# Experts with 128-slot tiles, two tiles in a turn

## The chip, the cores and the metric

The kernel runs on one core of a Trainium2 chip. The metric is the time of one execution on the device, in microseconds (us). Times of a kernel are given as the median of several runs; the profile comes from one further execution of its own.

## The reference

The input x is (8, 256, 32, 32): eight batches of 256 channels and 1024 positions. Layer 0 is a deformable convolutional attention with a small MLP for the position bias; layer 1 is an attention with sigmoid weights, followed by a mixture of experts. The change concerns the mixture most:

```python
x = x + conv_attention(group_norm(x))              # layer 0
t = tokens(x)                                      # 1024 tokens of 256 a batch
t = t + sigmoid_attention(layer_norm(t))           # layer 1
u = layer_norm(t)

logits = u @ router_w.T                            # 8 experts
probs = softmax(logits)
rw, re = top_k(probs, 2)
rw = rw / rw.sum(-1)
out = u
for e in range(8):
    h = gelu(u @ w1[e] + b1[e])
    out = out + combine[:, e] * (h @ w2[e] + b2[e])
t = t + out
```

`combine` is zero but for the two experts that each token has chosen. So each batch has 2 x 1024 pairs of a token and an expert. All arithmetic is fp32.

## The kernel before

**The outer order.** A Python loop writes out 8 x 64 turns (L1053), and a last pass, `in_order`, ties each engine to the order in which its instructions were written. Batch b of the loop does the position-bias MLP of batch b: in each turn two first layers (`first_layer`, on VectorE L451 or GpSimd L453), two second layers on TensorE (L466, with a relu on ScalarE L472 or a maximum on VectorE L474) and, every second turn, four rows of the third layer (L493). The tables that the first layer reads (`ta`, `nb`) are made by `terms`: every eighth turn (0, 8, 16, ...) four DMAs on the SyncE queue (L423, L424), three turns later a scaling (L427 on ScalarE, L428 on VectorE), one more turn later a small matmul (L434).

**What is woven in.** Each turn also advances, behind its MLP work:

- `prep` of the next batch: group norm, query projection, the depthwise convolution, offsets, sampling (L227 to L403);
- `attention` of layer 1, in two halves: `upper` starts at turn 53 of its own batch, `rest` runs in the next batch. `rest` ends with `route` (L780), which takes the logits to slots, and with sixteen scatters by GpSimd (L763), in turns 41 and after;
- `experts` (L867), the mixture of a batch; `mix` (L1038) says in which turns one step of it is made;
- `combine` (L937), 22 steps in consecutive turns from the one in which a mixture ends: sixteen gathers by GpSimd (L965) from the experts' rows `ys`, the weighted sums (L957), transposes (L948) and the output.

**The slots.** `route` counts, for each expert, how many tokens chose it, gives each expert as many tiles of SLOTS = 256 rows as it needs, and each pair a row in one of its expert's tiles. `need`, `ends`, `at`, `place`, `slot` are those steps; `which` and `whose` give `expert`, the expert of each tile. Whatever the counts are, TILES = (2048 + 8 x 255) // 256 = 15 tiles are enough, and always 15 are computed. The scatters write the normalized tokens to `xs`, of which there are two.

**One round.** `experts` is a generator with software pipelining. Step n of its loop (L890) makes, in this order: the second matmul of tile n - 2 (`yp`, L896, eight matmul records), the bias and the write to `ys` (L901, L904); the fetch of tile n + 2 (`xl`, L874); the load of the weights of tile n + 1 (`weights`, L877: one read of the expert's number into a register of SyncE, then w1 with b1, 257 KB, L880, and w2 with b2, 384 KB, L882); the first matmul of tile n - 1 (`hp`, L916, eight records) and its Gelu (`ht`, L922); four transposes of tile n (`tp`, L929) and their copy (`xg`, L931). In fp32 one matmul call makes two records in the trace. `wpool` holds three buffers for each weight. Before the loop there are two steps with fetches alone, so a mixture takes 19 steps.

**When.** The mixture of batch b is made in the loop of batch b + 2: at turns 24 and 26 and at odd turns from 27 on but for 35, 37, 39, 61 and 63, which are sixteen steps; the last three fall in batch b + 3, at turns 3, 7 and 9. Batches 0 and 1 have no mixture steps, and turns 3 and 7 of batch 2 have none. In batch 7 mixture 5 is made at odd turns and those divisible by three from 11 to 37. Mixture 6 begins in turns 62 and 63 and goes on while `rest` of batch 7 is made without an MLP beside it; mixture 7 comes after the last scatter and is made beside the combine of batch 6. The combine of batch 7 ends the program.

**Memory.** `low` (eleven buffers of 128 x 512) serves `xl`, `xg`, `ht`, `yt` and others; constants come as one tile `cs` of NCST columns, 799.5 KB, at the start.

Of the kernel before, what the change touches and what calls it, by code (L numbers as in the profile page):

```python
# [27 lines left out]
SLOTS = 256  # L28
TILES = (2 * N + E * (SLOTS - 1)) // SLOTS

# [8 lines left out]
    ("ident", 128), ("gavg", 128), ("base", 512), ("basef", 128),  # L39
    ("gq", 1), ("cx", 1), ("cy", 8), ("rev", 64),  # L40
    ("ones", 128), ("before", 128), ("full", 256), ("tiles", (E - 1) * TILES), ("form", 12),
# [53 lines left out]
def tile_conv_attn_hybrid(ctx: ExitStack, tc: tile.TileContext, x, par, qw, w1, w2_, cst, out):  # L95
# [9 lines left out]
    wpool = ctx.enter_context(tc.tile_pool(name="w", bufs=3))  # L105
# [105 lines left out]
    xss = [nc.dram_tensor(f"xs{n}", [TILES * SLOTS, C], F32, kind="Internal").ap() for n in range(2)]  # L211
# [15 lines left out]
    def prep(b, xb, st):  # L227
# [41 lines left out]
        for t in range(KS * KS):  # L269
# [9 lines left out]
        oa = one.tile([P, 2, NJ], F32, name="oa")  # L279
        nc.scalar.activation(  # L280
            oa.rearrange("p k (y x) -> p k y x", x=8), oc.rearrange("p (y k) x -> p k y x", k=2), AF.Gelu
        )
# [4 lines left out]
        for g in range(2):  # L287
            for c in range(2):
                nc.tensor.matmul(
                    op.rearrange("p (c k g j) -> p c k g j", c=2, k=2, g=2)[:, c, :, g, :],  # L290
                    lhsT=pw[:, 2 * g + c : 2 * g + c + 1].to_broadcast([P, P]), rhs=oa, start=True, stop=True,
                )
        opf = psum("opf")
        nc.tensor.matmul(
            opf[:, 0:128].rearrange("p (k j) -> p k j", k=2),
# [6 lines left out]
        nc.vector.scalar_tensor_tensor(gk[:, 0:512], gk[:, 0:512], 4.0, base, ALU.mult, ALU.add)  # L302
# [7 lines left out]
        fl = one.tile([P, 2 * NJ], F32, name="fl")  # L310
# [9 lines left out]
        fr = one.tile([P, 2, 64], F32, name="fr")  # L320
# [22 lines left out]
        hx = one.tile([P, 256], F32, name="hx")  # L343
# [238 lines left out]
    def attention(b, st, o, rt):  # L582
# [152 lines left out]
        def rest():  # L735
# [21 lines left out]
            yield from route(lqs, rt)  # L757
# [22 lines left out]
    def route(lqs, rt):  # L780
# [6 lines left out]
        revv = rev.rearrange("p (m e) -> p m e", e=E)  # L787
# [14 lines left out]
        def pick(name):  # L802
# [28 lines left out]
        nc.tensor.matmul(cnt, lhsT=cst_("ones"), rhs=sums, start=False, stop=True, skip_group_check=True)  # L831
        need = one.tile([P, E, E, 4], F32, name="need")
        nc.vector.tensor_tensor(
            need, cnt[:, 8, :].unsqueeze(1).unsqueeze(3).to_broadcast([P, E, E, 4]),
            cst_("full").rearrange("p (e f n) -> p e f n", e=E, f=E), ALU.is_gt,
        )
        nc.vector.tensor_reduce(ends[:, 1:9], need.rearrange("p e f n -> p e (f n)"), AX.X, ALU.add)
        for c in range(2):
# [4 lines left out]
            at, ends[:, 0:8].unsqueeze(1).to_broadcast([P, 8, E]), float(SLOTS), cnt[:, 0:8, :], ALU.mult, ALU.add  # L843
        )
        place = one.tile([P, 2, 8], F32, name="place")
        for c, oh in enumerate((oh1, oh2)):
# [5 lines left out]
        which = one.tile([P, TILES, E - 1], F32, name="which")  # L852
        nc.vector.tensor_tensor(
            which, ends[:, 1:8].unsqueeze(1).to_broadcast([P, TILES, E - 1]),
            cst_("tiles").rearrange("p (t e) -> p t e", e=E - 1), ALU.is_le,
# [11 lines left out]
    def experts(b, rt):  # L867
        xs = rt["xs"]
        yv = dram.tile([TILES * SLOTS, C], F32, name="ys")
        tiles = {}  # L870

        def fetch(t):
            xl = low("xl")
            nc.sync.dma_start(out=xl, in_=xs[t * SLOTS : (t + 1) * SLOTS, :].rearrange("(s p) c -> p s c", p=P))  # L874
            tiles[t] = [None, None, xl]

        def weights(t):  # L877
            e = nc.sync.value_load(rt["expert"][0:1, t : t + 1], min_val=0, max_val=E - 1)
            f1 = wpool.tile([P, 2 * C + 2], F32, name="w1")
            nc.sync.dma_start(out=f1, in_=w1[bass.ds(e, 1)].rearrange("e p c -> (e p) c"))  # L880
            f2 = wpool.tile([P, 3 * C], F32, name="w2")
            nc.sync.dma_start(out=f2, in_=w2_[bass.ds(e, 1)].rearrange("e p c -> (e p) c"))  # L882
            tiles[t][0:2] = f1, f2
# [4 lines left out]
        weights(0)  # L888
        yield
        for n in range(TILES + 2):  # L890
            if n >= 2:
                _, f2, ht = tiles.pop(n - 2)
                yp = psum("yp").rearrange("p (s c) -> p s c", s=2)
                for s in range(2):
                    for f in range(2):
                        nc.tensor.matmul(  # L896
                            yp[:, s, :], lhsT=ht[:, f, s * P : (s + 1) * P], rhs=f2[:, f * C : (f + 1) * C],
                            start=(f == 0), stop=(f == 1),
                        )
                yt = low("yt")  # L900
                nc.vector.tensor_tensor(  # L901
                    yt, yp, f2[:, 2 * C :].unsqueeze(1).to_broadcast([P, 2, C]), ALU.add
                )
                nc.sync.dma_start(  # L904
                    out=yv[(n - 2) * SLOTS : (n - 1) * SLOTS, :].rearrange("(s p) c -> p s c", p=P), in_=yt
                )
            if n + 2 < TILES:
                fetch(n + 2)
            if n + 1 < TILES:
                weights(n + 1)  # L910
            if 1 <= n <= TILES:
                f1, _, xg = tiles[n - 1]
                hp = psum("hp").rearrange("p (f i) -> p f i", f=2)
                for f in range(2):
                    for k in range(2):
                        nc.tensor.matmul(  # L916
                            hp[:, f, :], lhsT=f1[:, k * C + f * P : k * C + (f + 1) * P], rhs=xg[:, k, :],
                            start=(k == 0), stop=(k == 1),
                        )
                ht = low("ht")  # L920
                for f in range(2):
# [307 lines left out]
```

## Time and profile before

| | us |
|---|---|
| median of 3 runs | 3216.83 |
| lowest, highest | 3212.77, 3220.61 |
| the profiled execution, its own time | 3218.55 |
| its span, first to last instruction | 3216.8 |

The mean granted TensorE clock was 0.974 of full speed. By the view of busy time in stretches, the batches of the loop took 278, 337, 368, 376, 379, 375, 379 and 392 us, after a start of 73; the end, after turn 63 of batch 7, took 260 us.

| group | count | busy us | mean ns |
|---|---|---|---|
| L466 second MLP layer, TensorE | 8192 | 1026.8 | 611 |
| L493 third MLP layer, TensorE | 4096 | 506.5 | 613 |
| L896 `yp`, TensorE | 960 | 241.8 | 396 |
| L916 `hp`, TensorE | 960 | 229.4 | 382 |
| L929 `tp`, TensorE | 480 | 73.9 | 277 |
| L922 `ht`, ScalarE | 240 | 100.8 | 471 |
| L901 `yt`, VectorE | 120 | 82.6 | 688 |

Matmuls are pipelined, so the mean of one record is longer than the distance of two starts; busy time counts overlapping records once. The trace moved 281.20 MB by DMA in all, 87 GB/s on average.

### The profile page before, as it was taken

How to read it: one execution, taken by the hardware profiler on the slowest of the kernel's cores; microseconds unless marked ns; L12 is line 12 of the kernel's file. 1: busy time of each engine (PE TensorE's matmuls, PEld its weight loads, DVE VectorE, ACT ScalarE, POOL GpSimd, SP SyncE). 2: the span in 40 equal slices, each digit the busy share in tenths (PEclk: the TensorE clock that was granted, in tenths of full speed). 3: DMA queues.
4: the chain of work that ended last, by engine and by line, in shares of the span. 5: the costliest groups of instructions: out<-in, count | busy, mean ns of one | idle time of the engine just before them, and what ended most of it. 6: DMA issues, size and time to landing. Idle time of an engine off the chain costs nothing. (4 is left out here: it accounts for less than half of the span.)

```text
span 3216.8 us, 50328 instructions
## 1 busy us (share of the span) xinstructions
PE 2928.8 (91%) x19468; PEld 1465.1 (46%) x19468; DVE 2173.7 (68%) x2996; ACT 1841.1 (57%) x2435; POOL 1547.5 (48%) x945
## 2 busy tenths in 40 slices
PE   3888998899999998999989999999999999988986
PEld 2223343334545454554535445354544546523765
DVE  4898678967785787756876587757777464586122
ACT  3666565656566556655566566655566566545322
POOL 2546344744464454634555365543646343364123
PEclk7999999999999999999999999999999999999998
DMA  3311101210344123432335224441234333532277
GB/s 100 89 32 45 21 19 27 69 29 19 85 122 129 32 65 98 136 91 50 87 88 145 55 61 103 117 133 33 66 90 141 81 84 97 147 96 64 66 248 235
DMA packets 421567, 281.20 MB, mean 87 GB/s; under 512 B 283088, under 2 KB 378064, under 8 KB 421328
## 3 DMA queue, kind: packets, MB, share of 16 engines
q1 hardware_dynamic: 408752, 242.80, 28.4%
q0 software_dynamic: 12288, 33.57, 3.4%
q8 instruction: 153, 2.51, 0.3%
q10 hardware_dynamic: 288, 1.62, 0.1%
q14 instruction: 86, 0.70, 0.1%
HBM read 204.51 MB, written 73.40 MB: 86 GB/s over the span
## 5 line engine op out<-in xcount | busy, mean ns | idle before, releaser
L453 POOL TENSOR_TENSOR h<-ta,nb 128x1024 f32<-128x1024 f32 x512 | 1060.7, 2073 | 1122.9 <-PE h2p L466 1052.8
L466 PE MATMUL h2p<-h,pr__97 64*64 64x512 f32 x8192 | 1026.8, 611 | 118.8 <-DVE h L474 86.8
L474 DVE TENSOR_TENSOR h<-h2p,nc 128x1024 f32<-128x1024 f32 x512 | 624.2, 1219 | 518.0 <-PE h2p L466 512.4
L472 ACT ACTIVATE h<-h2p,pr__97 128x1024 f32<-128x1024 f32 x512 | 569.7, 1113 | 516.0 <-PE h2p L466 514.9
L451 DVE TENSOR_TENSOR h<-ta,nb 128x1024 f32<-128x1024 f32 x512 | 765.3, 1495 | 0.7 <-ACT ta L427 0.5
L458 ACT ACTIVATE h<-h 128x1024 f32<-128x1024 f32 x512 | 536.8, 1049 | 82.8 <-POOL h L453 82.7
L466 PEld LDWEIGHTS h2p<-h,pr__97 64*64 64x64 f32 x8192 | 256.1, 133 | 639.9 <-issue 303.6
L493 PE MATMUL sim<-h,pr__97 128*32 128x512 f32 x4096 | 506.5, 613 | 0.0
L493 PEld LDWEIGHTS sim<-h,pr__97 128*32 128x32 f32 x4096 | 108.6, 111 | 375.4 <-issue 375.4
L896 PE MATMUL yp<-w,ht 128*128 128x256 f32 x960 | 241.8, 396 | 18.7 <-ACT tn L630 10.7
L701 PE MATMUL ap<-qt,tn 128*128 128x256 f32 x1024 | 250.5, 388 | 0.5 <-ACT nc L439 0.5
L715 PE MATMUL vp<-tt,sg 128*128 128x256 f32 x1024 | 243.3, 381 | 0.3 <-ACT sg L706 0.3
L922 ACT ACTIVATE ht<-hp,w 128x256 f32<-128x256 f32 x240 | 100.8, 471 | 239.9 <-PE hp L916 200.6
L916 PE MATMUL hp<-xg,w 128*128 128x256 f32 x960 | 229.4, 382 | 6.0 <-ACT gk L299 2.8
L965 POOL DMA_INDIRECT gs<-ys,slot x128 | 139.1, 1087 | 193.2 <-DMA ys<-yt 57.8
L701 PEld LDWEIGHTS ap<-qt,tn 128*128 128x128 f32 x1024 | 185.2, 190 | 88.5 <-issue 55.9
L896 PEld LDWEIGHTS yp<-w,ht 128*128 128x128 f32 x960 | 178.8, 195 | 85.1 <-issue 31.8
L715 PEld LDWEIGHTS vp<-tt,sg 128*128 128x128 f32 x1024 | 193.2, 190 | 33.2 <-issue 6.9
L901 DVE TENSOR_TENSOR yt<-yp,w 128x512 f32<-128x512 f32 x120 | 82.6, 688 | 176.6 <-PE yp L896 137.9
L916 PEld LDWEIGHTS hp<-xg,w 128*128 128x128 f32 x960 | 183.0, 191 | 33.3 <-ACT gk L299 3.7
L763 POOL DMA_INDIRECT xs<-ut,slot x128 | 166.9, 1304 | 47.9 <-DVE slot L850 26.2
L276 DVE SCALAR_TENSOR_TENSOR oc<-qp,pr__97,oc 128x128 f32<-128x128 f32 x280 | 168.7, 603 | 7.2
(264 smaller groups left out, 2550.6 us busy)
## 6 DMA issues: line engine op xcount, KB each, us to landing
w<-in_w SPq DMA_DIRECT2D x120, 384.0 KB, 3.9
ta<-fd SPq DMA_DIRECT2D x128, 256.0 KB, 5.5
w<-in_w SPq DMA_DIRECT2D x120, 257.0 KB, 3.2
xl<-xs SPq DMA_DIRECT2D x120, 256.0 KB, 3.0
ys<-yt SPq DMA_DIRECT2D x120, 256.0 KB, 2.3
nb<-fd SPq DMA_DIRECT2D x128, 128.0 KB, 5.2
xb<-in_x SPq DMA_DIRECT2D x8, 1024.0 KB, 7.9
x<-in_x SPq DMA_DIRECT2D x8, 1024.0 KB, 8.5
```

The source lines that it names most:

```text
L276: nc.vector.scalar_tensor_tensor(oc, tap, dw[:, t : t + 1], oc, ALU.mult, ALU.add)
L451: nc.vector.tensor_tensor(h1, a, b, ALU.max)
L453: nc.gpsimd.tensor_tensor(h1, a, b, ALU.subtract)
L458: nc.scalar.activation(h1, h1, AF.Relu)
L466: nc.tensor.matmul(h2p[gs, r, :], lhsT=par_("w2")[rs, gs], rhs=h1[rs, g].rearrange("p y x -> p (y x)"), start=True, stop=True, tile_positi ...
L472: nc.scalar.activation(h2, h2p, AF.Relu, bias=par_("cb2"))
L474: nc.vector.tensor_tensor(h2.rearrange("p r (y x) -> p r y x", x=W), h2p.rearrange("p r (y x) -> p r y x", x=W), nc_.unsqueeze(3).to_broad ...
L493: nc.tensor.matmul(sim[32 * q : 32 * q + 32, :], lhsT=par_("z3")[:, 15 - m : 47 - m], rhs=h2s[2 * u + q // 2][:, q % 2, :], start=False, s ...
L701: nc.tensor.matmul(ap[:, u, :], lhsT=tn[:, k, m0 : m0 + P], rhs=qt[:, k, quarter(q)], start=(k == 0), stop=(k == 1),)
L715: nc.tensor.matmul(vp[:, i, :], lhsT=sg_[:, u, i * P : (i + 1) * P], rhs=tt[:, 2 * mp + u, :], start=(first and u == 0 and i == 0), stop=( ...
L896: nc.tensor.matmul(yp[:, s, :], lhsT=ht[:, f, s * P : (s + 1) * P], rhs=f2[:, f * C : (f + 1) * C], start=(f == 0), stop=(f == 1),)
L916: nc.tensor.matmul(hp[:, f, :], lhsT=f1[:, k * C + f * P : k * C + (f + 1) * P], rhs=xg[:, k, :], start=(k == 0), stop=(k == 1),)
```

## The change

SLOTS becomes SMALL = 128 for batches 0 to 6 and LARGE = 256 for batch 7. With 128 rows a tile, at most (2048 + 8 x 127) // 128 = 23 tiles are needed. `experts` now makes *rounds* of LARGE = 256 rows: `several` = 2 tiles of 128 each in batches 0 to 6, which are twelve rounds; one tile of 256 in batch 7, which are fifteen rounds as before. In a round of two tiles:

- `fetch` and the write of `ys` stay at 256 rows, one DMA each;
- `weights` is called once for w1 and once for w2, and each call reads the number of each tile's expert and loads its weights: four register reads and four weight DMAs a round, where there were one and two;
- `hp` is made for each tile: sixteen records of 128 columns for eight of 256, and four Gelus of 128 x 128 for two of 128 x 256;
- `yp` has eight records as before; each half of the rows has its own tile's w2, and the bias comes from both.

The pools become `w1pool` and `w2pool` with two buffers each, of two tiles' weights. w2 of round n is loaded in step n (it was step n - 1), w1 of round n + 1 at the end of step n, behind `hp` and Gelu of round n - 1. A mixture has 16 steps: `mix` leaves out turn 59 and, in the next batch, turns 3 and 7.

To make room, constants are smaller and are broadcast when they are read (`base`, `rev`, `ones`, `full`, `tiles`), and tiles of `prep` and `route` are used again (`oa` is `oc`, `fl` and `hx` lie in `gk`, `fr` in `ft`, `need` and `which` in a PSUM bank).

```diff
-SLOTS = 256
-TILES = (2 * N + E * (SLOTS - 1)) // SLOTS
+LARGE, SMALL = 256, 128
+def tiles_of(slots):
+    return (2 * N + E * (slots - 1)) // slots
+TILES = tiles_of(SMALL) + 1
+ROWS = max(tiles_of(LARGE) * LARGE, TILES * SMALL)
...
-    wpool = ctx.enter_context(tc.tile_pool(name="w", bufs=3))
+    w1pool = ctx.enter_context(tc.tile_pool(name="w1", bufs=2))
+    w2pool = ctx.enter_context(tc.tile_pool(name="w2", bufs=2))
...
-        nc.scalar.activation(
-            oa.rearrange("p k (y x) -> p k y x", x=8), oc.rearrange("p (y k) x -> p k y x", k=2), AF.Gelu
-        )
+        nc.scalar.activation(oc, oc, AF.Gelu)
+        oa = oc.rearrange("p (y k) x -> p k y x", k=2)
...
-        nc.vector.scalar_tensor_tensor(gk[:, 0:512], gk[:, 0:512], 4.0, base, ALU.mult, ALU.add)
+        for c in range(2):
+            gc = gk[:, c * 256 : (c + 1) * 256].rearrange("p (n j) -> p n j", j=NJ)
+            nc.vector.scalar_tensor_tensor(
+                gc, gc, 4.0, base[:, c * NJ : (c + 1) * NJ].unsqueeze(1).to_broadcast([P, 4, NJ]), ALU.mult, ALU.add
+            )
...
-            yield from route(lqs, rt)
+            yield from route(lqs, rt, LARGE if b == NB - 1 else SMALL)
...
-        nc.vector.tensor_reduce(ends[:, 1:9], need.rearrange("p e f n -> p e (f n)"), AX.X, ALU.add)
+        many = one.tile([P, E], F32, name="many")
+        nc.vector.tensor_reduce(many, need, AX.X, ALU.add)
+        nc.vector.tensor_tensor(
+            part(1), many.unsqueeze(1).to_broadcast([P, E, E]), cst_("upto").rearrange("p (e f) -> p e f", e=E), ALU.mult
+        )
+        nc.vector.tensor_reduce(ends[:, 1:9], part(1), AX.X, ALU.add)
...
+        slots_ = LARGE if b == NB - 1 else SMALL
+        several = LARGE // slots_
+        rounds = -(-tiles_of(slots_) // several)
...
-        def weights(t):
-            e = nc.sync.value_load(rt["expert"][0:1, t : t + 1], min_val=0, max_val=E - 1)
-            f1 = wpool.tile([P, 2 * C + 2], F32, name="w1")
-            nc.sync.dma_start(out=f1, in_=w1[bass.ds(e, 1)].rearrange("e p c -> (e p) c"))
-            f2 = wpool.tile([P, 3 * C], F32, name="w2")
-            nc.sync.dma_start(out=f2, in_=w2_[bass.ds(e, 1)].rearrange("e p c -> (e p) c"))
-            tiles[t][0:2] = f1, f2
+        def weights(t, pool, width, w, name):
+            f = pool.tile([P, 2, width], F32, name=name)
+            for u in range(several):
+                n = t * several + u
+                e = nc.sync.value_load(rt["expert"][0:1, n : n + 1], min_val=0, max_val=E - 1)
+                nc.sync.dma_start(out=f[:, u, :], in_=w[bass.ds(e, 1)].rearrange("e p c -> (e p) c"))
+            return f
...
-            if n + 1 < TILES:
-                weights(n + 1)
+            if n < rounds:
+                second[n] = weights(n, w2pool, 3 * C, w2_, "w2")
...
                 for f in range(2):
-                    for k in range(2):
-                        nc.tensor.matmul(
-                            hp[:, f, :], lhsT=f1[:, k * C + f * P : k * C + (f + 1) * P], rhs=xg[:, k, :],
-                            start=(k == 0), stop=(k == 1),
+                    for u in range(several):
+                        us = slice(u * slots_, (u + 1) * slots_)
+                        for k in range(2):
+                            nc.tensor.matmul(
+                                hp[:, f, us], lhsT=f1[:, u, k * C + f * P : k * C + (f + 1) * P], rhs=xg[:, k, us],
+                                start=(k == 0), stop=(k == 1),
+                            )
+                tokens_[n - 1] = ht = low("ht")
+                for f in range(2):
+                    for u in range(several):
+                        us = slice(u * slots_, (u + 1) * slots_)
+                        nc.scalar.activation(
+                            ht[:, f, us], hp[:, f, us], AF.Gelu, bias=f1[:, u, 2 * C + f : 2 * C + f + 1]
                         )
...
+            if n + 1 < rounds:
+                first[n + 1] = weights(n + 1, w1pool, 2 * C + 2, w1, "w1")
...
-            due = i in (24, 26) or i > 26 and i % 2 and i not in (35, 37, 39, 61, 63)
+            due = i in (24, 26) or i > 26 and i % 2 and i not in (35, 37, 39, 59, 61, 63)
         elif of == b - 3:
-            due = i in (3, 7, 9)
+            due = i == 9
```

## The prediction

> **What bounds the kernel now.** First the page's busy line and slices:
>
> ```profile
> PE 2928.8 (91%) x19468; PEld 1465.1 (46%) x19468; DVE 2173.7 (68%) x2996; ACT 1841.1 (57%) x2435; POOL 1547.5 (48%) x945
> ...
> PE   3888998899999998999989999999999999988986
> ...
> DMA  3311101210344123432335224441234333532277
> ```
>
> TensorE is the bound by its share, and DMA is idle for two thirds of the time except in the last two slices. An average says nothing of one turn, though, so I cut the trace into turns. L466 has 8192 records, sixteen for each of 512 turns; the first of each sixteen starts a turn. I then set turns with and without an expert step side by side, in the view of busy time by stretches (columns: us, PE, PEld, DVE, ACT, POOL, clock, DMA share, GB/s):
>
> ```profile
> 658.51:671.46 12.95, 11.33 (x76) 4.03 (x72) 8.01 (x6) 10.10 (x15) 7.23 (x3) 1.00 0.16 32
> 1396.03:1415.12 19.09, 16.48 (x97) 8.54 (x93) 6.44 (x7) 10.13 (x17) 3.82 (x2) 0.91 0.40 120
> 705.40:739.07 33.67, 29.12 (x199) 11.01 (x195) 26.10 (x41) 15.76 (x18) 12.90 (x8) 0.90 0.14 25
> 1073.02:1107.30 34.28, 32.75 (x235) 17.08 (x231) 25.82 (x43) 19.20 (x24) 12.40 (x8) 1.00 0.05 16
> 1263.74:1283.65 19.91, 14.96 (x126) 3.86 (x125) 19.09 (x36) 11.15 (x14) 9.24 (x5) 1.00 0.22 43
> 2812.91:2844.67 31.76, 25.46 (x170) 12.42 (x169) 23.05 (x41) 14.80 (x20) 8.75 (x6) 0.95 0.27 62
> ```
>
> These are turns 59-60 of batch 1 (no step) and batch 3 (step at 59); turns 3-8 of batch 2 (none) and batch 3 (steps at 3 and 7); turns 35-39 of batch 3 (none) and batch 7 (steps at 35, 36, 37). The reader should see that a step's 3.6 us of TensorE work (turn 31: 2.38 us in batch 1, 5.97 us in batch 3) is not what its turn costs. At 59 the step adds 6.1 us. At 3 and 7 two steps together add 0.6 us, because turns 4 and 8 then wait for other things: without the steps they took 8.50 and 7.90 us, with them 5.71 and 4.05.
>
> Last, the SyncE queue, which issues all of a round's DMAs in order:
>
> ```profile
> 1381.60 0.38 SPq L904 DMA_DIRECT2D ys<-yt  x1
> 1382.03 0.47 SPq L874 DMA_DIRECT2D xl<-xs  x1
> 1383.62 0.36 SPq L880 DMA_DIRECT2D w<-in_w  x1
> 1384.23 0.36 SPq L882 DMA_DIRECT2D w<-in_w  x1
> 1384.69 0.59 SPq L423 DMA_DIRECT2D ta<-fd  x1
> ```
>
> From the end of xl (1382.50) to the end of the first weight DMA (1383.98) is 1.48 us: reading the expert's number into a register, then the issue. The 120 such pieces have a median of 1.43 us and run from 1.08 to 2.16.
>
> **The change part by part.** The sum is made against the profiled execution: 3218.55 us, 1.7 us above the shown median of 3216.83.
>
> *Three rounds fewer in seven batches.* Batches 0 to 6 run 12 rounds for 15. In `mix` this strikes turn 59 of batches 2 to 6 and turns 3 and 7 of batches 3 to 7; mixture 5 in batch 7 ends at turn 33 instead of 37; mixture 6 at the end has 9 rounds left after the attention, not 12.
>
> (a) Turns 59-60: 19.09, 19.14, 19.15 us (batches 3, 4, 6) and 17.47, 17.48 (2, 5) against 12.95: 18.40 + 9.05 = 27.5 us. Batch 1 shows what those turns are without the step, so what grows in turn 60 (8.87 for 8.28) is counted.
>
> (b) Turns 3-8: 0.61 us each in batches 3 to 6, 0.08 in batch 7 (33.74): 2.5 us.
>
> (c) Batch 7, turns 35-39: 31.76 - 19.91 = 11.9 us at most; but the combine moves four turns forward, into 33 to 36, and in batch 3 single combine turns cost up to 1.8 us (turn 11: 7.35 for 5.51). I take 10, bounds 6 and 12.
>
> (d) The end. Mixture 7's first fetch was issued at 3109.91, after mixture 6's last write. It also needs the last of sixteen scatters (L763), issued at 3097.61 and 0.96 long, plus 3.3 us to land: 3102. So 7.9 us is all that can be won. Three rounds at the old pace (4.65 us, yp starts 3079.84 to 3084.49 to 3089.14) are 14. But SyncE's round grows: ys 0.38 + xl 0.47 + four reads and issues at 1.43 = 6.6 us (5.2 to 9.5 by the bounds of that piece), where it was 0.38 + 0.47 + 1.43 + 0.60 = 2.9. It takes TensorE's place as the bound there; five such rounds after 3064 give about 10 to 11 us back of the 14. I take 4 us, bounds 0 and 7.9.
>
> DMA itself: a round moves 2 x (257 + 384) + 256 + 256 KB = 1.84 MB. The stretch 3115-3150 ran at 294 GB/s with a share of 0.91, which extrapolates to 323 GB/s and 5.7 us a round, below SyncE's 6.6. [...]
>
> *Half as wide hp matmuls.* Eight records of 256 columns become sixteen of 128; yp keeps its eight. The hp group is 229.4 us / 960 = 0.239 us a record. The nearest row with a new 128x128 weight at each 128-column matmul is L374:
>
> ```profile
> 968.48 1.47 PE L493 MATMUL sim<-h,pr__97 128*32 128x512 f32 x12
> 969.88 3.84 PE L374 MATMUL kv<-wt,xt 128*128 128x128 f32 x32
> 1380.34 1.89 PE L916 MATMUL hp<-xg,w 128*128 128x256 f32 x8
> ```
>
> Starts inside lie 0.1115 us apart for L374, 0.216 for L916: 16 x 0.1115 - 8 x 0.216 = +0.056 us a round. By the groups' means (L374: 32.4 / 256 = 0.127) it is +0.11. The third bound, weight loads not hidden at all (192 ns each), is excluded: 32 of them fit in 3.84 us. (e) 72 rounds, mixture 6's apart, since SyncE covers it: 4.0 us lost, at most 8. [...]
>
> *Four Gelus of 128x128 for two of 128x256.* L280's 0.31 us each: 1.24 for 0.84, +0.4 us on ScalarE, which is busy 57%: after the step of turn 55 its next relu (L472) ended at 1384.93, and TensorE's next L466 began at 1386.33, 1.4 us later. Nothing; if that cover were gone, 0.4 x 72 = 29 us. I keep it out of the sum, with 2 us in the range.
>
> *Weights.* Two buffers for three. w2 is now loaded two rounds ahead, w1 only after the Gelu of the same step has read the buffer's old biases. That wait is new on SyncE's queue; behind it stand the next round's write, fetch and w2, the combine's xc and out, and after turns 31, 47 and 55 the terms (ta, nb). In the bulk a round is two turns, some 10 us, and 6.6 us of queue plus 4 to 5 us of landing end within two rounds. In mixture 7 a round is 4.3 us: from Gelu's end, 1.4 us to issue and 4.1 to land (L880's median after 3050) make 5.5; hp comes 4.3 + 1.8 = 6.1 later. The cover is 0.6 us. (f) 1.5 us lost; at the longest landing seen, 5.4, it is 0.7 us a round, so 0 to 6 with some of it absorbed.
>
> *Terms behind weights.* ta/nb of turn 56 stood behind turn 55's weights: issued to 1389.26, landing 5.5 us later, used by ScalarE at 1399.38, so 4.6 us of slack. Now two more pieces (2.9 us) and 641 KB more in front (2.0 us at 323 GB/s): 4.9. Late by 0.3; at 32 and 48 the window is some 5 us longer. ScalarE's queue behind it is `tn` and the relus, for which TensorE waits. (g) 1 us lost, 0 to 6.
>
> *Smaller constants.* cst shrinks from 799.5 to 383.5 KB. TensorE's first instruction waits for the parameter load until 9.82; 2.9 MB land by then, so 0.43 MB is about 1.2 us (0 to 2). (h) 1.2 gained.
>
> *Rest.* Gelu in place, base in two adds, two small vector steps more in `route`: eight times a few tenths on VectorE beside TensorE work; two adds of 0.3 for one of 0.69 in the uncovered start. Nothing; without cover under 0.5 us a batch.
>
> Sum: 27.5 + 2.5 + 10 + 4 - 4.0 - 1.5 - 1 + 1.2 = 38.7 us. 3218.55 - 38.7 = **3180**.
>
> **Rivals.** *TensorE work counts in full*: 21 rounds x 3.59 us, less 4.0, is 71 us: 3147. For it: 91% busy. Against: turns 3-8. 12%.
>
> *The dropped work is refilled and the end gains nothing*: (d) zero and (c) 6, (f) and (g) at 6, (e) at 8, the Gelus 2: 27.5 + 2.5 + 6 - 8 - 6 - 6 - 2 + 1.2 = 15: 3203 or a little above. 12%, within the range's upper edge.
>
> *SyncE becomes the bound in the bulk* (slower). Each of turns 35, 51 and 59 in batches 2 to 6 takes a table loaded behind eight DMAs. If terms come late by more than 38.7 / 15 = 2.6 us at each, all is lost; at 4.2 us (the longest landing, 9.4 us, for 5.5, with the 0.3) it is 63 us of cost: 3243. For: one queue, and it more than doubles per round. Against: 35 and 51 have slack to spare, and SyncE is idle for 934 us waiting on yt alone. 10%.
>
> That the change does less than it says (a 13th round needed) I exclude: at most 23 tiles are needed, and 12 rounds hold 24.
>
> **Numbers.** 66% for the forecast. Best end: 27.5 + 2.5 + 12 + 7.9 + 2 - 4 = 48: 3171; I go down to 3162 for part of the first rival, up to 3203 for the second. About 0.2% (6 us) is what a measurement here can tell from no change: within that only a stretch of the two upper rivals, 4%; slower 10%; faster 86%.
>
> **What would show it.** Turn 59 near 4.1 us and turn 60 near 8.9; turns 3-8 near 33.7; hp records starting 0.11 us apart; in mixture 6's last rounds SyncE's issues following each other without a pause, 6 to 7 us a round, and mixture 7's first fetch some 4 us earlier against the last scatter (12.3 us after its issue now, 8 then). I am wrong if the ScalarE scaling of ta in turns 35, 51 or 59 starts after idle time that a DMA ended, if hp in mixture 7 waits for w1, if mixture 6's rounds keep 4.65 us, or if turn 60 grows by as much as turn 59 shrinks.

## The result, and the profile after

| | before | after |
|---|---|---|
| median (lowest, highest), us | 3215.30 (3212.77, 3220.61), 4 runs | 3157.13 (3154.65, 3163.42), 4 runs |
| ratio, 95% interval | | 0.982 [0.980, 0.984] |
| the profiled execution, us | 3218.55 | 3163.42 |
| its span | 3216.8 | 3161.7 |

The change makes the kernel 58 us faster by the medians. The prediction was 3180 with a range of 3162 to 3203: the direction was right, the size was too small, and the time lies 5 us below the range. The profiled execution of after is the slowest of its four; pair against pair the profile has to account for 55.1 us, and the term-by-term comparison below is made against that, not against the 58.2 of the medians.

The busy line and the slices of the page after, to be held against those of before:

```profile
PE 2859.6 (90%) x19720; PEld 1417.3 (45%) x19720; DVE 2169.9 (69%) x2999; ACT 1824.7 (58%) x2533; POOL 1549.8 (49%) x945
...
PE   3889898899999999999999999999999999978976
...
DMA  3212101211246125541246223561256325631387
```

TensorE is busy 69 us less, VectorE 4, ScalarE 16, and GpSimd 2 more. The page thus still says "TensorE, 90%", and can't say where the 55 us went. So the same cut as in the prediction is made: the first of each sixteen records of the second MLP layer (now L478) starts a turn. The view of busy time by stretches, kernel after (us, PE, PEld, DVE, ACT, POOL, clock, DMA share, GB/s): turns 59-60 of batch 1 and of batch 3, turns 3-8 of batch 3 and of batch 7, turns 35-39 of batch 7.

```profile
661.21:674.17 12.96, 11.34 (x77) 4.04 (x73) 8.00 (x6) 10.11 (x15) 7.23 (x3) 1.00 0.16 32
...
1394.64:1406.08 11.44, 10.72 (x77) 3.95 (x73) 6.10 (x6) 8.60 (x14) 4.29 (x2) 1.00 0.28 78
1068.37:1101.99 33.62, 29.01 (x198) 10.97 (x194) 26.08 (x41) 15.76 (x18) 13.04 (x8) 0.90 0.15 25
2542.64:2572.16 29.52, 26.57 (x195) 10.17 (x191) 21.42 (x31) 15.76 (x18) 12.11 (x6) 0.94 0.17 28
2768.07:2793.40 25.33, 17.73 (x126) 4.60 (x125) 24.45 (x43) 14.12 (x17) 20.21 (x13) 0.87 0.30 68
```

The reader should see three things. Turns 59-60 of batch 3 were to become those of batch 1 (12.95 us before, 12.96 now), and became 1.5 us shorter than that. Turns 3-8 of batch 3 came out at the 33.7 that was forecast; those of batch 7 were forecast at the same 33.7 and are 4 us below it. And by the last two columns the DMA share is 0.15 to 0.30 in all of them, at 25 to 78 GB/s.

What turn 59 was worth is plain from the timeline of batch 3 (`bp` are four transposes of the attention in TensorE, `tn` is ScalarE's copy of them). Before (start, us, engine, line, operation, in brackets the idle time ahead of it):

```profile
1396.03 1.95 PE L466 MATMUL h2p<-h,pr__97 64*64 64x512 f32 x16
...
1400.51 1.05 ACT L630 COPY tn<-bp 128x512 f32<-128x512 f32 x2
1401.14 3.60 PE L896 MATMUL yp<-w,ht 128*128 128x256 f32 x8 [2.14 <-ACT tn L630]
1404.58 1.89 PE L916 MATMUL hp<-xg,w 128*128 128x256 f32 x8
...
1406.84 1.95 PE L466 MATMUL h2p<-h,pr__97 64*64 64x512 f32 x16
```

After:

```profile
1394.64 1.95 PE L478 MATMUL h2p<-h,pr__100 64*64 64x512 f32 x16
...
1396.52 1.09 PE L639 MATMUL bp<-cs,tt 128*128 128x128 f32 x8
...
1397.55 1.95 PE L478 MATMUL h2p<-h,pr__100 64*64 64x512 f32 x16
```

Before, TensorE had only `bp` between the two MLP layers and the step; then `yp` waited 2.14 us for ScalarE's copy `tn`, ran at half clock (3.60 us for eight records that take 1.99 elsewhere; the granted clock was 0.50 for 3.41 us there), and the step's `hp` and `tp` followed. That is 10.81 us for a turn which takes 2.90 without the step, though a step holds 3.6 us of TensorE work by the prediction's own row.

The pair of profiles by the prediction's terms (profiled after less before, us):

| term | predicted | measured |
|---|---|---|
| (a) turns 59-60, batches 2 to 6 | -27.5 | -35.2 |
| (b) turns 3-8, batches 3 to 7 | -2.5 | -10.3 |
| (c) batch 7 but for turns 3 to 8 | -10 | -10.1 |
| (d) and (f) the end, from the last turn's start | -2.5 | -1.2 |
| (e), (g) and all else in the loop | +5 | +3.8 |
| (h) the start | -1.2 | -2.1 |
| sum | -38.7 | -55.1 |

A half-clock piece is a stretch, mostly of 3.41 us, in which the granted clock was 0.50 (see the last section). In the fifth row stand also those pieces that fell otherwise in turns the change doesn't touch: batches 0 and 1, which have no step at all, are 4.8 us longer than before. Not all of that is the clock: turn 54 of batch 1 takes 9.35 us in the three profiles with the old code (before, move59, before12) and 11.1 in ten of the eleven with the new, for a reason that wasn't looked for.

### The profile page after: what moved, and what is told of

It reads as the page before. It is cut to its first block, busy times and chain, and to the rows that moved or that the text cites. A ratio compares the mean times of both kernels' runs of the same rounds, so it can differ in the third digit from the quotient of the medians.

```text
span 3161.7 us, 51886 instructions
## 1 busy us (share of the span) xinstructions
PE 2859.6 (90%) x19720; PEld 1417.3 (45%) x19720; DVE 2169.9 (69%) x2999; ACT 1824.7 (58%) x2533; POOL 1549.8 (49%) x945
## 5 line engine op out<-in xcount | busy, mean ns | idle before, releaser
L478 PE MATMUL h2p<-h,pr__100 64*64 64x512 f32 x8192 | 1028.7, 610 | 138.3 <-DVE h L486 113.1
L478 PEld LDWEIGHTS h2p<-h,pr__100 64*64 64x64 f32 x8192 | 253.8, 133 | 664.6 <-issue 293.3
L505 PE MATMUL sim<-h,pr__100 128*32 128x512 f32 x4096 | 520.9, 628 | 0.0
L947 ACT ACTIVATE ht<-hp,w 128x128 f32<-128x128 f32 (+1 forms) x366 | 108.6, 377 | 194.4 <-PE hp L939 169.2
L921 PE MATMUL yp<-w,ht 128*128 128x256 f32 x792 | 195.9, 390 | 13.7 <-DMA w<-in_w 8.2
L939 PE MATMUL hp<-xg,w 128*128 128x128 f32 (+1 forms) x1464 | 196.0, 286 | 7.4 <-ACT gk L307 2.8
L921 PEld LDWEIGHTS yp<-w,ht 128*128 128x128 f32 x792 | 144.1, 191 | 72.7 <-issue 33.7
L926 DVE TENSOR_TENSOR yt<-yp,w 128x512 f32<-128x512 f32 x99 | 68.3, 690 | 150.9 <-PE yp L921 137.3
```

What stands on the lines that cost most here:

```text
L478: nc.tensor.matmul(h2p[gs, r, :], lhsT=par_("w2")[rs, gs], rhs=h1[rs, g].rearrange("p y x -> p (y x)"), start=True, stop=True, tile_positi ...
L505: nc.tensor.matmul(sim[32 * q : 32 * q + 32, :], lhsT=par_("z3")[:, 15 - m : 47 - m], rhs=h2s[2 * u + q // 2][:, q % 2, :], start=False, s ...
L921: nc.tensor.matmul(yp[:, s, :], lhsT=ht[:, f, s * P : (s + 1) * P], rhs=f2[:, s * several // 2, f * C : (f + 1) * C], start=(f == 0), stop ...
L939: nc.tensor.matmul(hp[:, f, us], lhsT=f1[:, u, k * C + f * P : k * C + (f + 1) * P], rhs=xg[:, k, us], start=(k == 0), stop=(k == 1),)
```

## The experiments

Three groups of four kernels; the kernels of a group ran on one chip beside the kernel before, whose medians were 3219.42, 3225.46 and 3226.40 us. So ratios are compared between groups, and microseconds only within one or between profiles.

| kernel | median us | ratio, 95% interval |
|---|---|---|
| move59 | 3192.80 | 0.9919 [0.9902, 0.9935] |
| before12 | 3138.24 | 0.9755 [0.9737, 0.9772] |
| after15 | 3244.83 | 1.0081 [1.0064, 1.0097] |
| large | 3223.72 | 1.0014 [1.0005, 1.0024] |
| to61 | 3174.45 | 0.9840 [0.9823, 0.9856] |
| sched37 | 3169.04 | 0.9830 [0.9813, 0.9848] |
| w2early | 3166.34 | 0.9813 [0.9796, 0.9830] |
| best | 3165.31 | 0.9817 [0.9791, 0.9842] |
| again | 3175.64 | 0.9848 [0.9829, 0.9867] |
| oneread | 3165.33 | 0.9810 [0.9787, 0.9833] |
| oneread-w2 | 3164.24 | 0.9808 [0.9791, 0.9824] |
| reads8 | 3179.03 | 0.9864 [0.9837, 0.9891] |

**Is it the place or the work?** move59 is the kernel before with one number changed: as many steps, as many rounds.

```diff
-            due = i in (24, 26) or i > 26 and i % 2 and i not in (35, 37, 39, 61, 63)
+            due = i in (24, 26) or i > 26 and i % 2 and i not in (35, 37, 39, 59, 63)
```

> The kernel before with one thing changed: the expert step of turn 59 is made in turn 61 instead (still 15 rounds of 256 rows). Theory A (a step in turn 59 costs 6.3 to 7.9 us, its own 3.6 us and a wait for a PSUM bank and a halved clock behind it; in turn 61 it costs its 3.9 us): 15 to 17 us less than before, ratio 0.995. Theory B (what came beyond the forecast came from the new weights, buffers and constants, and a step costs the same in 59 as elsewhere): no change.

It is 26.6 us faster than before by the medians. Its profiled execution is the slowest of four, 13.7 us below that of before, and there turns 59 to 61 give 15.7, as theory A expected. The other three executions are 11 to 14 us shorter than it; where, isn't known, as they have no trace. Turn 59 gives 6.3 us in the two batches where the profile before had no half-clock stretch in it and 7.9 in the three where it had one. Turn 60 takes back 0.25, turn 61 3.9. The same two stretches of batch 3 in move59, turns 59-60 and turn 61:

```profile
1395.28:1406.71 11.43, 10.71 (x76) 3.95 (x72) 6.10 (x6) 8.60 (x14) 4.28 (x2) 1.00 0.03 12
1406.71:1414.41 7.70, 7.70 (x46) 5.49 (x45) 3.05 (x3) 6.15 (x7) 1.91 (x1) 1.00 0.06 20
```

Turns 59-60 are those of after, to 0.01 us, with the old code of a round. In turn 61 TensorE is busy for all 7.70 us: the step costs its own 3.9 us and no stall. So of the 35.2 us of term (a) somewhat under half, 15.7, is the bad place, which any schedule could have left; the other 19.4 is the struck work, 3.9 us a batch.

**How many rounds, and what a round costs.** before12 is the kernel before with twelve rounds instead of fifteen in batches 0 to 6, so that three tiles of each are left out, and the turns of after in `mix` (first edit). after15 makes fifteen of the new rounds (second edit) and large uses one tile of 256 in all batches (third), both with the turns of before in `mix`.

```diff
-        for n in range(TILES + 2):
+        rounds = TILES if b == NB - 1 else 12
+        for n in range(rounds + 2):
...
-        rounds = -(-tiles_of(slots_) // several)
+        rounds = 15
...
-        slots_ = LARGE if b == NB - 1 else SMALL
+        slots_ = LARGE
```

> The kernel before with 12 rounds of 256 rows for 15 in batches 0 to 6, in the turns of the changed kernel; three tiles are left out, and the gather reads their rows' tokens from the last row made. Single weights, full-width matmuls, old constants. Theory A (all of the gain is the struck rounds): 55 to 62 us less than before, at least as fast as the changed kernel, since the end runs at TensorE's 4.65 us a round. Theory B: some 39 us less, as the forecast had it.

> The changed kernel with 15 rounds of two tiles in batches 0 to 6 and the old turns: twice the weights and half-wide matmuls, but no round saved. Theory A: +6 us (0.056 x 105 rounds), -2 us (start), and the end SyncE-bound: nine rounds of mixture 6 at 6.6 for 4.65 us, +17, and mixture 7 waiting for w2, +3: about 24 us more than before, nearly all of it behind turn 63 of batch 7. Theory B (the new code gains by itself): less than before. If SyncE's queue were late in the bulk as well, turns 35, 51 and 59 would grow and the sum be above 50 us.

> The changed kernel with 256 slots, one tile in a round and 15 rounds in all batches, in the old turns: only the new constants, the reused tiles and the split and later weight loads remain. Theory A: -2 us at the start, +3 us at the end (mixture 7 waits for w2), within 5 us of before. Theory B: 15 to 20 us less than before.

Measured against the kernel before of the group: before12 -81.2, after15 +25.4, large +4.3 us. The last two are near what was expected; before12 went some 20 us beyond theory A. By the profiles it is 24.2 us below after: 9.9 at the end, 0.5 at the start and 14.0 in the loop, of which 5.0 are batches 0 and 1, without any step. From these: without struck rounds the new kernel is no faster at all, it is slightly slower. Two tiles' weights in a round cost 21.1 us for 105 rounds (after15 less large); by the profiles 5.2 of it in the loop and 14.2 at the end. Where no half-clock piece falls differently, most turns with a step are 0.057 us longer in after15 than in large, which is the halved `hp` of term (e); turn 29, which has a mixture's first `hp`, is 0.36 us longer in batches 3 to 6. That the loop's sum comes near what (e) makes of its rounds is chance: batch 0, without a step, is 5.1 us shorter, batch 7 6.7 longer. In no batch of after15 does the scaling of the tables in turns 35, 51 and 59 come late: term (g) is zero, and SyncE doesn't bound the bulk.

At the end before12 has 248.3 us, after 258.2, before 259.4, after15 279.6. Striking three rounds of mixture 6 is worth 11 us there if a round costs what it did (before12), and in this profile the new code takes 10 of them back: 5.8 by the first `yp` of mixture 7, with two tiles' weights a round, and 3.8 within mixture 7, whose rounds have one tile as before but the new order of loads.

**Why turn 59 beat its twin.** The first explanation was that in batch 1 GpSimd and ScalarE run late in turn 59 because turn 57 has no step either; to61 is the kernel after with that step moved to 61.

```diff
-            due = i in (24, 26) or i > 26 and i % 2 and i not in (35, 37, 39, 59, 61, 63)
+            due = i in (24, 26) or i > 26 and i % 2 and i not in (35, 37, 39, 57, 59, 63)
```

> The kernel after, with the step of turn 57 made in turn 61 (batches 2 to 6), so that neither 57 nor 59 has a step, as in batch 1. Theory A (turn 59 is 2.90 us and not batch 1's 4.08 because the step in turn 57 holds TensorE long enough for GpSimd and ScalarE to get ahead): turns 57 to 60 become batch 1's 2.57, 5.58, 4.08, 8.87 for 5.59, 3.73, 2.90, 8.53, together +0.35 us a batch, and turn 61 gains a step (3.80 to about 7.7): +4.2 us a batch, +21 us in all. Theory B (the step in 57 has no part in it; turn 59 stays at 2.90 for another reason): 57 and 58 give -1.2 us, 59 and 60 nothing, 61 +3.9: +13 us in all. The record of turn 59 decides: 4.08 or 2.90.

Turns 57-58, 59-60 and 61 of batch 3 in to61; in after they are 9.31, 11.44 and 3.80 us:

```profile
1379.48:1385.65 6.17, 5.73 (x53) 1.35 (x49) 6.07 (x9) 4.27 (x5) 5.23 (x4) 1.00 1.17 159
1385.65:1397.50 11.85, 10.94 (x77) 3.80 (x73) 9.96 (x7) 9.01 (x14) 6.62 (x3) 1.00 0.01 1
1397.50:1404.81 7.31, 7.31 (x49) 5.41 (x48) 2.90 (x3) 5.81 (x6) 1.91 (x1) 1.00 0.00 1
```

Theory A falls: 59-60 grow by 0.4, not to batch 1's 12.96, so the step in 57 is not what shortens them. Both sums were wrong too (+21 and +13 expected): moved, the step costs 3.5 in turn 61 and gives 3.1 in 57-58, +0.8 us a batch with the 0.4 of turns 59-60. What batch 1 lacks beside it are the steps of turns 53 and 55 and of all earlier turns; which of them sets the 1.5 us stays open.

**Turns 3 and 7.** sched37 is after with the steps of turns 24 and 26 made in turns 3 and 7 of the next batch.

```diff
-            due = i in (24, 26) or i > 26 and i % 2 and i not in (35, 37, 39, 59, 61, 63)
+            due = i > 26 and i % 2 and i not in (35, 37, 39, 59, 61, 63)
...
-            due = i == 9
+            due = i in (3, 7, 9)
```

> The kernel after, with the mixture of batches 0 to 4 begun two steps later: turns 24 and 26 have none, and turns 3 and 7 of the next batch have one again; the number of rounds is the same. Theory A (a step in turns 3 and 7 costs little, because turns 4 and 8 wait for other work anyway; 0.6 us where no half-clock window falls differently, 2.5 where one does, 4.2 in batch 7): +0.6 to +4.2 us a batch there, and the two steps that now have fetches alone, turns 27 and 29, and the one with transposes alone, turn 31, give back -0.4, -4 and -2 (turn 29 is 3.19 us in batch 1, where it has no step, and 7.69 after): net -2 to -6 us a batch, -10 to -30 us in all, predicted -20. Theory B (the 10.3 us that turns 3 to 8 lost with the change were the price of the two steps, 2.1 us a batch, in whatever clock): the steps cost at least 2.1 us a batch and more where SyncE now has four reads a round in place of two: net about 0 to -10 us.

Turns 3-8 of batches 3, 4 and 7 in sched37, which has the steps:

```profile
1068.31:1102.71 34.40, 32.87 (x250) 17.82 (x247) 25.88 (x43) 19.70 (x28) 12.46 (x8) 1.00 0.12 39
1433.26:1467.62 34.36, 32.77 (x250) 17.79 (x246) 25.84 (x43) 19.70 (x28) 12.62 (x8) 1.00 0.13 39
2529.13:2562.96 33.83, 32.24 (x247) 17.27 (x243) 22.86 (x34) 19.70 (x28) 14.16 (x8) 1.00 0.17 50
```

In after those of batch 4:

```profile
1440.01:1471.78 31.77, 27.22 (x198) 10.81 (x194) 26.10 (x41) 15.76 (x18) 12.63 (x8) 0.95 0.14 25
```

The two steps cost 0.8 us in batch 3, 2.6 in batch 4, 4.3 in batch 7 (+0.8 and +2.4 in 5 and 6): 10.9 in all, as much as the change had won there. The rows explain the spread. With steps TensorE idles 1.5 to 1.6 us and the clock is 1.00. Without them it idles 4.6 us in the stretch and half-clock pieces come: two in batch 3 (0.90), one in batch 4 (0.95), a difference of 1.85 us. In batch 7 there is no `prep`, so turn 8 takes 3.79 us, with TensorE busy throughout, instead of 7.9, of which it idles 1.98: there was no such wait for a step to hide in.

Turns 27 to 33 gave back 9.0 us a batch, and turn 32 took 2.6 of it (7.1 in batch 2): 6.4 net, the sum that was expected (1.7 in batch 2). But over batches 2 to 6 the loop is only 12.0 us shorter than in the unchanged kernel's second profile (again), since turn 57 takes 0.44 a batch and turn 11, now with a half-clock piece in each of batches 3 to 6, 10.1 in all; and batch 7 is 9.1 longer, 4.3 of it the steps (against after). The medians say -6.6 across two groups. So A's prices of the turns hold and its -10 to -30 us doesn't: theory B's range has the time.

**The end of the program.** w2early has the two halves of each weight buffer serve in turn in batch 7, so that w1 and w2 of the next round are both asked for ahead of `hp`; best is that with sched37.

```diff
+            if several == 1:
+                if t % 2 == 0:
+                    pairs[name] = pool.tile([P, 2, width], F32, name=name)
+                e = nc.sync.value_load(rt["expert"][0:1, t : t + 1], min_val=0, max_val=E - 1)
+                nc.sync.dma_start(out=pairs[name][:, t % 2, :], in_=w[bass.ds(e, 1)].rearrange("e p c -> (e p) c"))
+                return pairs[name][:, t % 2 : t % 2 + 1, :]
...
+            if several == 1 and n + 1 < rounds:
+                first[n + 1] = weights(n + 1, w1pool, 2 * C + 2, w1, "w1")
+                second[n + 1] = weights(n + 1, w2pool, 3 * C, w2_, "w2")
```

> The kernel after; in batch 7, where a round has one weight of each kind, the two halves of each weight buffer serve in turn (four buffers for two), and w1 and w2 of round n + 1 are both read in step n ahead of hp, as in the kernel before. Theory A (the end gave back 3.4 us in mixture 7 because yp waits for a w2 that is asked for in its own step): the stretch from mixture 7's first fetch to its last yp goes from 76.4 to about 73.0 us, and the time by -3 us. Theory B (the stretch is paced by SyncE's issue and the scatter of the rows, whatever the order): the wait moves from yp to hp or to the transposes, 0 us. The loop before turn 62 of batch 7 stays within 1 us but for half-clock windows.

> Both of the last two edits together. Theory A of both: -23 us against the kernel after, a ratio to the kernel before near 0.975. If the two share a cause, or sched37's gain is half-clock windows that fall elsewhere, less: 0.980 to 0.982.

The ends of all four kernels of this group were longer than that of after, 264 to 271 us for 258, the wrong way for w2early. The cause wasn't in mixture 7: SyncE's instructions, most of which elsewhere take 0.02 to 0.5 us, followed each other in steps of 0.70 us for 16 us in the last rounds of mixture 6. The third group therefore had the unchanged kernel with it, and two edits of SyncE's work: oneread keeps the expert's number in its register for the second weight, reads8 makes each read twice.

```diff
-                e = nc.sync.value_load(rt["expert"][0:1, n : n + 1], min_val=0, max_val=E - 1)
+                e = read.pop(n, None)
+                if e is None:
+                    e = nc.sync.value_load(rt["expert"][0:1, n : n + 1], min_val=0, max_val=E - 1)
+                    read[n] = e
```

> The kernel after, unchanged, beside the three others on the same chip. In four kernels of the last group (to61, sched37, w2early, best), all on one chip, SyncE's instructions followed each other in steps of 0.70 us for some 16 us in mixture 6's last rounds, which the first profile of the kernel after doesn't show, and their ends were 6 to 13 us longer than its 258.2. Theory A (that is a state of the run or of the chip, not of the edits): here the unchanged kernel shows it too, or none of this group's kernels does. Theory B (the edits moved SyncE's instructions so that it comes): the unchanged kernel has 258 us of end and no such stretch, wherever it runs.

> The kernel after with one read of the expert's number for each tile, kept in its register for both weights: two reads a round of two tiles in place of four, one for two in batch 7. A read takes SyncE 0.6 to 1.25 us from the start of the load to the start of the address sum. Theory A (SyncE's issue paces the last rounds of mixture 6): these go from 5.6 to 7.7 us to about 5, the last yp of mixture 6 comes some 6 us sooner, and in mixture 7 a w2 is asked for 0.6 us sooner, -2: -5 to -9 us against the unchanged kernel on this chip, all of it behind the last turn. Theory B (the transfers or TensorE pace them, and SyncE only stands in the chain because it issues them): within 2 us of the unchanged kernel.

> The last edit together with the early w1 and w2 of w2early. Theory A (yp of mixture 7 waits for w2): a further -2 to -3 us against oneread, from mixture 7's first fetch to its last yp 73 us. Theory B (the wait moves to hp or the transposes): within 1 us of oneread.

> The kernel after with each read of an expert's number made twice in batches 0 to 6: eight reads a round. Theory A (SyncE's issue paces mixture 6's last rounds, and nothing else): four reads more at 0.6 us are +2.4 us for each of some 6 to 8 rounds there, +14 to +19 us, and the loop keeps its time within 3 us. Theory B (SyncE bounds the loop's rounds as well, where two steps follow two turns apart): more than +30 us. Theory C (transfers pace them): within 3 us.

The unchanged kernel shows the stretch as well, with an end of 268.2 us: theory A. In again, four pieces of the chain that ended last (start, us), the busy time of the stretch, and the waits from 3020 to 3050 us (us in total, times, longest; "remote" is a release that the profile puts down to nothing on this core):

```profile
3038.11 0.70 issue
3038.80 0.70 issue
3039.50 0.70 SPq L927
3040.22 1.38 SPq L906
```

```profile
3028.00:3044.00 16.00, 8.13 (x34) 6.63 (x33) 0.00 (x0) 1.73 (x5) 10.55 (x11) 0.65 0.65 209
```

```profile
DVE yt L926 <- remote: 16.6, 1, 16.6
ACT ht L947 <- remote: 9.3, 1, 9.3
```

The same 16 us in the first profile of after:

```profile
3028.00:3044.00 16.00, 12.54 (x63) 10.12 (x64) 2.14 (x5) 3.52 (x11) 12.04 (x14) 0.89 1.02 363
```

So it is no property of the edits, and w2early's microseconds are compared with again's: -4.0 at the end. From mixture 7's first `yp` to its last it took 67.0 us in again, 63.6 in w2early, 64.2 in oneread, 62.3 in oneread-w2 (63.3 before, 66.2 in the first profile of after). That is theory A of w2early, -3.4 for -3, and of oneread-w2, 1.9 less than in oneread and 2.7 less at the end, where -2 to -3 was expected; by the medians the two differ by 1.1, less than the intervals can tell. The chain of waits shows it. After, from 3060 to 3090 us, in mixture 7 (shares by line, then start, us, what ended last):

```profile
by line: DMA w<-in_w 32.0%; PE yp L921 22.5%; issue 21.5%; PE hp L939 20.3%; ACT ht L947 5.3%; SPq L906 3.9%; SPq L900 2.5%; ACT xg L959 2.0%; DVE xc L984 1.6%; PE tp L957 1.5%; SPq L907 0.6%; DVE yt L926 0.2%; ACTq L947 0.1%; SPq L927 0.0%
...
3068.91 0.47 SPq L900
3069.42 0.56 SPq L906
3070.48 4.96 DMA w<-in_w
3075.58 1.97 PE yp L921 x8
```

In oneread-w2, over the same 30 us, no transfer is in the chain:

```profile
by line: PE hp L958 43.8%; PE yp L937 43.6%; ACT ht L966 10.9%; issue 1.9%; PE tp L976 1.5%; ACTq L966 0.2%
...
3079.99 1.99 PE yp L937 x8
3081.99 1.74 PE hp L958 x8
3083.75 0.48 ACT ht L966
```

oneread is 10.3 us below again by the medians, for 5 to 9 expected, but not where theory A has it: its end is 4.3 us shorter than again's, 2.8 of it in mixture 7, and mixture 6's last `yp` comes only 0.4 us sooner after the last turn's start, for 6 expected, since the stalled stretch lies on those very rounds. reads8 makes that `yp` 6.8 us later, for 14 to 19 expected, with a loop 2.9 shorter, 4.6 of it in batch 0, which has no round; its median is 3.4 above again's, less than the intervals can tell. Ahead of the stretch two rounds take 7.1 and 8.3 us, for 5.6 and 6.7 in again, where theory A has 2.4 more; in the stretch two `yp` are 18.8 apart, for 12.4, and whether that comes of the reads isn't known. More issue time on SyncE does lengthen those rounds, then, by some two thirds of what theory A makes of it, and theories B and C fall. That fewer reads would shorten them is not shown, and how much of the rounds' growth is issue and how much the doubled transfers stays open.

Of the complete kernels oneread-w2 is the best of its group, 11.4 us below again by the medians; the two intervals just fail to touch. sched37 and w2early together (best) did not add up: 0.9817 for 0.975 expected.

## Why the prediction was too small, by its own steps

Of the 16.4 us that the sum was too small by, (a) and (b) make 15.5. None of the prediction's signs of being wrong came; the first line of what would show it, turn 59 near 4.1 us and turn 60 near 8.9, did not hold for turn 59 (2.90; turn 60 is 8.53). The miss is small beside what two groups of runs differ by: beside the kernel before of its own group, again gained 50.8 us by the medians, not 58.2, which from 3216.83 would lie inside the range. But there too turns 59-60 of batches 2 to 6 are 35.2 us shorter than in the profile before and turns 3-8 11.8; it is the end that is 8.8 longer, not 2.5 shorter.

**(a) failed in its size**, at the sentence "Batch 1 shows what those turns are without the step". What the turns cost before was read rightly (but for a slip: the first three differences make 18.53, not 18.40), though without the stall and the half-clock stretch behind it. What they would become was not: batch 1 has no steps in the turns before either, and in its turn 59 (4.08 us) `bp` and the next second layer wait 0.33 and 0.24 us for ScalarE, whose relu starts 2.93 us into the turn, for 1.41 in batch 3's (2.90 us). How short the turn can become was to be read from its own TensorE work: a second layer (1.95 us, with overlap) and `bp` (1.09) fill the 2.90 us without a gap. 7.7 us were missed.

**(b) failed in its size**, at "0.61 us each in batches 3 to 6, 0.08 in batch 7 (33.74)". 33.67 was one row, batch 2's, and it held two half-clock pieces (clock 0.90); batches 4 and 6 drew one fewer. For batch 7 the row of a batch with `prep` was subtracted from one without, and its own turn 8 would have told: -4.2 for -0.1. Together 7.8 us.

**(c)** came out right, partly by luck: turns 35-39 gave 6.4 us for the 10, and the other turns of batch 7, outside 3 to 8, the rest of 10.1; in again it is 8.2.

**(d) and (f)** have the mechanism, as far as the runs show it, and (d) lies within its bounds in the first profile. SyncE's queue took TensorE's place in mixture 6's last rounds: these ran at 5.6 to 7.7 us for the 6.6 worked out, and SyncE's pieces make 48% of the chain of after for the stretch 3022 to 3056, beside 26% of weight transfers, where before, in the last rounds up to 3116, 68% were `yp` and `hp`:

```profile
by line: DMA w<-in_w 26.3%; SPq L906 24.8%; SPq L907 14.4%; issue 14.0%; PE yp L921 6.0%; SPq L900 5.6%; PE hp L939 4.8%; SPq L927 3.5%; DVE yt L926 2.1%; ACT ht L947 1.1%; ACTq L947 0.1%
```

```profile
by line: PE yp L896 35.4%; PE hp L916 33.0%; DMA w<-in_w 11.3%; ACT ht L922 9.3%; issue 3.9%; SPq L874 3.2%; DVE yt L901 2.3%; SPq L878 1.5%; SPq L904 1.2%; SPq L880 0.2%; ACTq L922 0.2%; DVEq L901 0.1%
```

By reads8, though, added issue time lengthens a round by only two thirds of what this makes of it. Mixture 7's first fetch came 5.84 us after the last scatter, for 8 forecast and 12.30 before: -6.5 us. The scatter itself came 1.5 later, mixture 7 took 3.4 longer, for 1.5 in (f), and what follows it 0.3 longer: -1.2. In (f) the wrong transfer was named. `hp` doesn't wait for w1 in this profile (once, 0.7 us, in again); `yp` waits for w2, between 3065 and 3140 us five times (us in total, times, longest):

```profile
PE yp L921 <- DMA w<-in_w: 5.6, 5, 1.5
```

"w2 is now loaded two rounds ahead" left out that with two buffers its load waits for the bias of the round two before, and then stands behind that round's write and fetch.

**(e)** was right: +0.06 us a round (16 records in 1.948 us for eight in 1.890). **(g)** cost nothing: no scaling of a table was late, not even with fifteen new rounds.

**(h)** can't be called shown. The start shrank by 2.1 us, but by 0.9 in move59 and 2.6 in before12, both with the old constants.

**Rivals.** TensorE's work in full (3147) is refuted by turns 3-8, where two steps were worth 0.8 to 2.6 us in four of five batches; in turns 59 and 61, though, a step is worth its work or more. That the end gains little was nearly so (1.2 us), but the loop refilled nothing. SyncE as the bound of the bulk is refuted by after15, whose turns with a step lost `hp`'s 0.057 us against large and turn 29 0.36, and by reads8, whose batches 1 to 7 are 1.6 us longer than again's with eight reads a round.

## What to carry to other kernels

What a piece of work cost here was a property of the place where it was put: two steps, of some 3.6 us of TensorE work each, cost 0.8 us together in one place and a single one 7.9 in another, so move it before you make it smaller, and try that by itself. A twin row is a twin only if the turns before it are alike and the granted clock of both rows is the same; check that, and read from the engine's own work in the turn how short the turn can become. Where the last stage has only the mixture to do, count the queue that issues its transfers: there two tiles' weights a round and their new order took back 10 of 11 us, without the stalled stretch of the next section.

## What the runs showed of the hardware that had not been expected

The granted clock falls in pieces: 26 of the 30 in the loop and the end of the profile of after last 3.41 us, and all are at 0.50. In batches 3 to 6 they come in turns 4, 8, 11, 36 and 40, in which TensorE idled for 1.4 to 2.3 us by the mean of these batches. Which of several like turns gets one differs between kernels (of turns 11 in batches 3 to 6 those of 3 and 6 in after, of 4 and 6 in before) and between two profiles of one kernel: turn 11 of batch 3 is 10.04 us in after and 7.36 in again, with the same instructions. Batch 0, without a step, takes 274.4 to 279.7 us in the fourteen profiles. That the pieces make all of these 5.3 us wasn't shown; from before to after (277.9 to 279.4 us) the 1.5 us are those of turn 46, where after has one piece more. In the profile of after all pieces start on one grid of 3.413 us (to 0.002 us), and in the loop TensorE was busy for at most 1.75 us in the 3.41 us just before each (1.83 in before); of those stretches of the grid at full clock that no piece followed, none had under 1.53 (1.54 in before). So in the loop of these two profiles every piece had at least 1.58 us of TensorE's idle time in the stretch of the grid ahead of it, and no stretch at full clock with more than 1.88 was without a piece behind it: it counted where a turn's idle time fell on the grid. The grid's place differed between profiles: 2.45 us from the program's first instruction in after, 1.56 in before, 1.63 in again.

The stalled stretch: in again between 3027 and 3045 us, while GpSimd sent the last of its sixteen scatters (1.27 us apart, undisturbed), SyncE went on in steps of 0.70 us, VectorE started nothing for 16 us, and from 3028 to 3044 ScalarE was busy for 1.73 us and TensorE for 8.13, at a DMA share of 0.65, where the first profile of after has 3.52 and 12.54 us and a share of 1.02. In all eight profiles of the last two groups, the unchanged kernel's among them, two successive `yp` of mixture 6's last five rounds lie 12 to 19 us apart there (in oneread VectorE is held, 15.6 us in the chain); in the six profiles taken earlier none of these are more than 8 apart. With it the end of the unchanged kernel is 10.0 us longer (268.2 for 258.2, of which 0.8 are in mixture 7); whether it is also why the ratio was 0.982 at first and 0.985 in the third group, the timed runs can't say, as they have no trace. The kernel before has no profile in these two groups either; its medians there are 6 to 7 us above that of the first, so it may have the stretch too. The cause is open: with the stretch the instruction queues moved 2 packets from 3020 to 3060 us (w2early), without it 4 (after), and nothing here varied the scatters.
